# Two-layer transformer kernel: one DVE addition per rotation, key transposes in another PSUM pool, and a later place for the left factors of a seven-product multiplication

## The chip, the cores and the metric

The kernel runs on one core of a Trainium2 chip. The metric is the device time of one execution in microseconds, as the median of the runs shown. The engines have short names in the profile: PE is TensorE (matrix products), PEld its weight loads, DVE is VectorE, ACT is ScalarE, POOL is GpSimd, and SP is SyncE, whose queue issues all DMAs here.

## The reference

Two transformer layers over x of shape 4 x 256 x 256 (4 sequences, 256 positions, width 256), all in fp32. Each layer is `x = x + attention(layernorm(x))` followed by `x = x + ffn(layernorm(x))`.

```
# layer 0, attention: 16 query heads, 8 key/value heads of 128, window of 128
q, k, v = project(x)                       # per head: 256 -> 128
q, k = rms_norm(q), rms_norm(k)
q, k = rope(q), rope(k)                    # [x1*cos - x2*sin, x2*cos + x1*sin]
probs = softmax(mask(q @ k.T * scale));  out = (probs @ v) @ W_out
# layer 0, ffn: silu(x Wg) * (x Wu), keep the two largest of each four, times Wd
# layer 1, attention: 16 heads of 128, causal;  layer 1, ffn: silu(..)*(..), Hadamard transform, W2
```

What the change touches is the rotation and the key transpose in layer 0's attention, and the projections at the start of layer 1's attention.

## The kernel before, in words

**Stages.** The program runs `attention0`, `ffn0`, `attention1`, `ffn1` (lines 842 to 861), with overlaps at the seams. Layer 0's attention takes roughly the first 260 us, its FFN the time up to 367 us (the last products of it, `finish_ffn0`, run inside the next stage), layer 1's attention the time up to 660 us, and its FFN the rest.

**Units.** Each attention is cut into 16 units. In `attention0`, unit n belongs to sequence b = n // 4 and head group g = n % 4 (four query heads, two key heads, two value heads). `pipelined` (L301) runs six stages on them, each some steps behind the one before: `project` (no lag), `turn` (one step later), `score` (two), `split` (three), `join` and `attend` (four). So the step in which unit n is projected is also the one in which unit n-1 is turned and unit n-2 is scored.

**`project0` (L408)** multiplies the normalised input with the weights of a unit, for both halves t of the 256 positions. Each product of 128 x 512 lands in a PSUM tile `pj`, in the tag `half` of pool `ps2`, which has four buffers (L422). Two DVE multiplications read it, with the sines into `qs` and with the cosines into `qc` (L430); ACT squares it into `sq` (L435) and copies the values out (L437). After the products, DVE makes the rotation from two additions, one for each half of the 128 columns of a head (L441 and L442), and sums the squares (L443). POOL computes the reciprocal roots (L456 to L462) and scales the keys (L465). From unit 6 on (`by_dma`), POOL also splits the query words into two planes (L451) and a DMA transposes them (L453).

**`turn0` (L471)** brings queries and keys into transposed form. Up to unit 5 PE transposes the queries into a `half` tile (L478); from unit 6 on DVE copies the planes back (L485). The keys are always transposed by PE (L491) into a PSUM tile `tk` from `bank`, the tag of pool `ps1`, also with four buffers (L489), and ACT copies them out to `kT` (L492).

**Who else uses `bank`.** `probabilities` (L192) puts the scores `sc` there, one tile for each of a unit's four query heads, which DVE reads with a fused add-mask-and-maximum (L207) before ACT takes the exponentials (L217). `attend` (L374) takes two more for `av`, ACT copies them out (L388). A sequence's output projection `po` (L294) takes one, and a transposed input `tr_n` (L177) one.

**`attention1` (L656).** Each unit is projected with seven instead of eight block products (`seven_products`, L608): the left operand is the transposed input in four blocks and three combinations of them, which `left_of` (L588) makes with four DVE subtractions or additions (L596); the third of the seven products is the first to read a combination. The sums of the products are built by ACT copies (L613, L619, L622, L631) and DVE additions (L616, L625, L628). The four left operands are made in the first four units, in `project` (L659): unit b makes the operand of sequence b+1 and starts the normalisation of sequence b+2 (`normed`, L159, `by_dma`: DVE statistics and normalisation, two POOL instructions for the root, two POOL copies into planes, one transposing DMA issued by SP, two ACT copies out, L186), both before its own products.

**What sets the order.** Each engine executes its queue in order. The order within a queue is not that of the source: the build schedules the instructions of all engines by estimated readiness, subject to the dependencies, the free buffers and the order of the source. In the trace, for example, the products of unit 13 stand around the key transposes of unit 11. `tc.issue_after(ins)` adds one more constraint: instructions in its block come after `ins` on the same engine.

Of the kernel before, what the change touches and what calls it, by code (L numbers as in the profile page):

```python
# [24 lines left out]
ALU = mybir.AluOpType  # L25
# [23 lines left out]
def two_layers(ctx, tc, consts, tables, x, wq, wkv, wo, w_gate, w_up, w_down,  # L49
# [109 lines left out]
    def normed(b, factors=None, by_dma=False):  # L159

        mv, rstd = factors or moments(b)
        xnT = npool.tile([P, NC, T], F32, tag="xnT", name="xnT", bufs=4)
        if by_dma:
            planes = page_of_planes([P, NT, 2, D], "xpl")
        else:
            tr = bank([NC, T], "tr_n")
        for t in range(NT):
            cols = slice(t * P, (t + 1) * P)
            xn = npool.tile([P, D], F32, tag="xn", name="xn")
            last_of["norm"] = nc.vector.tensor_scalar(  # L170
                xn, xs[b * NT + t], mv[:, t, 0:1], rstd[:, t : t + 1], ALU.subtract, ALU.mult
            )
            if by_dma:
                copy_gpsimd(planes[:, t], xn.bitcast(U16).rearrange("p (n w) -> p w n", w=2))
                continue
            for c in range(NC):
                nc.tensor.transpose(tr[:, c, cols], xn[:, c * P : (c + 1) * P], ident)  # L177
        if not by_dma:
            nc.scalar.copy(xnT, tr)  # L179
            return xnT  # L180

        turned = page_of_planes([P, NT * 2 * NC, P], "xplT")
        nc.sync.dma_start_transpose(turned, planes.rearrange("p t w n -> p (t w n)"))
        for t in range(NT):
            cols = slice(t * P, (t + 1) * P)
            nc.scalar.copy(  # L186
                xnT[:, :, cols].bitcast(U16).rearrange("p c (n w) -> p c n w", w=2),
                turned[:, 4 * t : 4 * t + 4, :].rearrange("p (w c) n -> p c n w", w=2),
            )
        return xnT  # L190
# [125 lines left out]
    def attention0():  # L316
        with tc.tile_pool(name="attn0", bufs=2, reuse_waits="tile", side="right") as own:
            xnT, factors = {0: normed(0)}, {}


            cos_s = own.tile([P, NT, 2, HD], F32, name="cos_s", bufs=1)
            sin_s = own.tile([P, NT, 2, HD], F32, name="sin_s", bufs=1)
            with tc.issue_after(last_of["norm"].ins):
                for t in range(NT):
                    for tab, at in ((cos_s, 0), (sin_s, 256)):
                        src = angles[:, at + t * HD : at + (t + 1) * HD]
                        nc.vector.tensor_tensor(
                            tab[:, t], src.unsqueeze(1).to_broadcast([P, 2, HD]), scl, ALU.mult
                        )

            def project(n, _):
                b, g = divmod(n, 4)
                held = project0(own, xnT[b], g, cos_s, sin_s, n >= 6)
                if g == 1 and b + 1 < B:
                    factors[b + 1] = moments(b + 1)
                if g == 2 and b + 1 < B:
                    with tc.issue_after(last_of["qc"].ins):
                        xnT[b + 1] = normed(b + 1, factors[b + 1])
                return held

            def turn(n, held):
                rot, qT_planes, v, r = held
                return *turn0(own, rot, qT_planes), v, r

            def score(n, held):
                qT, kT, v, r = held
                ps = [
                    probabilities(
                        qT, kT, (2 * kk, 2 * kk + 1), mask0,
                        r[:, :, 2 * kk : 2 * kk + 2].rearrange("p t h -> p h t"),  # L350
                    )
                    for kk in range(2)
                ]
                return ps, v

            def split(n, held):
                ps, v = held
                return ps if n >= B * 4 - 3 else [
                    planes(p, own_planes) for p in ps
                ], v  # L360

            def own_planes(shape, name):
                return own.tile(shape, U16, tag="pl", name=name, bufs=4)

            def join(n, held):
                ps, v = held
                return [
                    transposed(ps[kk]) if n >= B * 4 - 3 else joined(ps[kk], ((
                        (nc.scalar.copy, slice(0, 2), last_of["exp"]),
                        (nc.scalar.copy, slice(0, 2), last_of["exp"]),  # L370
                    )[kk],)) for kk in range(2)
                ], v

            def attend(n, held):  # L374
                pTs, v = held
                zT = page("zT")
                for kk in range(2):
                    pT = pTs[kk]
                    av = bank([2, T], "av")
                    nc.tensor.matmul(  # L380
                        av, lhsT=v[:, 0, kk, :], rhs=pT[:, :, 0:T], start=True, stop=False,
                        skip_group_check=True,
                    )
                    nc.tensor.matmul(
                        av[:, :, P:T], lhsT=v[:, 1, kk, :], rhs=pT[:, :, T:],
                        start=False, stop=True, skip_group_check=True,
                    )
                    nc.scalar.copy(zT[:, 2 * kk : 2 * kk + 2, :], av)  # L388
                return zT

            def out(b, t, kept=False):
                def emit(done):
                    zTs = [done[4 * b + g] for g in range(4)]
                    if not kept:
                        project_out(bank([D], "po"), zTs, wo_sb, b, t)
                    else:
                        with tc.issue_after(last_of[0].ins):
                            project_out(half([D], "po"), zTs, wo_sb, b, t)
                return emit

            behind = {
                8: [out(0, 0)], 9: [out(0, 1)], 12: [out(1, 0)], 13: [out(1, 1)],
                17: [lambda _: xn_f.append(normed(0))],
                                19: [lambda _: xn_f.append(normed(1)), out(2, 0, True), out(2, 1, True), out(3, 0), out(3, 1)],
            }
            pipelined((project, turn, score, split, join, attend), (0, 1, 2, 3, 4, 4), behind, (0, 4, 3, 2, 1, 5))

    def project0(own, xnT, g, cos_s, sin_s, by_dma):  # L408
# [29 lines left out]
            rot.append((qc, qs, sq))  # L438
        for t, (qc, qs, sq) in enumerate(rot):

            nc.vector.tensor_tensor(qc[:, :, 0:64], qc[:, :, 0:64], qs[:, :, 64:], ALU.add)  # L441
            nc.vector.tensor_tensor(qc[:, :, 64:], qc[:, :, 64:], qs[:, :, 0:64], ALU.add)  # L442
            nc.vector.tensor_reduce(ss[:, t, :], sq, AX.X, ALU.add)  # L443
            rot[t] = qc
        qT_planes = None
# [22 lines left out]
            )  # L468
        return rot, qT_planes, v, r

    def turn0(own, rot, qT_planes):  # L471

        qT = page("qT")
        kT = own.tile([P, 2, T], F32, tag="kT", name="kT", bufs=3)
        for t, qc in enumerate(rot):
            cols = slice(t * P, (t + 1) * P)
            if qT_planes is None:
                tq = half([4, P], "tr_q")  # L478
                for j in range(4):
                    nc.tensor.transpose(tq[:, j, :], qc[:, j, :], ident)  # L480
                nc.vector.tensor_copy(qT[:, :, cols], tq)
            else:
                halves = qT_planes[:, 8 * t : 8 * t + 8, :]
                with tc.issue_after(last_of["mx"].ins):
                    nc.vector.tensor_copy(  # L485
                        qT[:, :, cols].bitcast(U16).rearrange("p j (c w) -> p j c w", w=2),
                        halves.rearrange("p (w j) c -> p j c w", w=2),
                    )
            tk = bank([2, P], "tr_k")  # L489
            for j in range(2):  # L490
                nc.tensor.transpose(tk[:, j, :], qc[:, 4 + j, :], ident)  # L491
            nc.scalar.copy(kT[:, :, cols], tk)  # L492
        return qT, kT
# [162 lines left out]
    def attention1(finish_ffn0):  # L656
        left = left1

        def project(n, _):  # L659
            g, b = divmod(n, 4)  # L660
            if g == 0 and b + 1 < B:
                left[b + 1] = left_of(xn1[b + 1])
            if g == 0 and b + 2 < B:
                xn1[b + 2] = normed(b + 2, by_dma=True)
            if b == 1 and 1 <= g < 3:
                load_group1(g + 1)
            return project1(left[b], gw[g])

        def score(n, held):
            qk, v = held  # L670
# [274 lines left out]
```

## Time and profile before

| | us |
|---|---|
| Median of 3 runs (lowest, highest) | 758.55 (758.15, 759.35) |
| The profiled execution, its own time | 761.02 |
| Its span, from the first to the last instruction | 759.2 |
| PE busy | 740.8 |
| DVE busy | 468.7 |
| ACT busy | 398.9 |
| POOL busy | 328.2 |
| DVE fused maximum on scores (L207), 256 instructions | 78.7 |
| POOL plane split of probabilities and inputs (L242), 54 | 80.1 |

A profile page gives busy times for an engine, the span in 40 slices with the busy share of each, the chain of work that ended last, and groups of instructions with their mean duration and the idle time before them. The views behind the page give waits ("engine, line, waited for: us in total, times, longest"), sums for any stretch of time, and the instructions in order of time ("start, us, engine, line, operation, output and input, shape, count, and in brackets the idle time before it and what ended it"). PE's matmuls are pipelined, so their durations overlap; what a matmul takes of PE's time is the distance from its start to the start of the next one. In this trace that distance, where nothing waits, is 0.429 us for a moving operand of 512 columns, 0.216 us for 256 and 0.112 us for 128 (medians). A `nc.tensor.matmul` in fp32 is two such instructions, a transpose one.

### The profile page before, as it was taken

How to read it: one execution, taken by the hardware profiler on the slowest of the kernel's cores; microseconds unless marked ns; L12 is line 12 of the kernel's file. 1: busy time of each engine (PE TensorE's matmuls, PEld its weight loads, DVE VectorE, ACT ScalarE, POOL GpSimd, SP SyncE). 2: the span in 40 equal slices, each digit the busy share in tenths (PEclk: the TensorE clock that was granted, in tenths of full speed). 3: DMA queues.
4: the chain of work that ended last, by engine and by line, in shares of the span. 5: the costliest groups of instructions: out<-in, count | busy, mean ns of one | idle time of the engine just before them, and what ended most of it. 6: DMA issues, size and time to landing. Idle time of an engine off the chain costs nothing. (4 is left out here: it accounts for less than half of the span.)

```text
span 759.2 us, 11685 instructions
## 1 busy us (share of the span) xinstructions
PE 740.8 (98%) x3980; PEld 602.5 (79%) x3980; DVE 468.7 (62%) x1428; ACT 398.9 (53%) x985; POOL 328.2 (43%) x475
## 2 busy tenths in 40 slices
PE   8999999998999999999989999999999999999998
PEld 5555556654666788888989999999998989899997
DVE  6999896699567515987655644464443447454433
ACT  2378886678558822222247555555555675415332
POOL 1588999779579301011116433343337645210000
PEclk9999999999999999999999999999999999999999
DMA  8724445426434050000433432342332222001100
GB/s 322 281 42 69 74 81 101 79 51 118 68 65 77 1 221 16 15 15 14 125 70 66 124 62 42 75 121 42 43 70 43 43 43 42 2 0 22 24 12 28
DMA packets 121611, 53.31 MB, mean 70 GB/s; under 512 B 114768, under 2 KB 116944, under 8 KB 120784
## 3 DMA queue, kind: packets, MB, share of 16 engines
q1 hardware_dynamic: 121552, 52.57, 30.1%
q8 instruction: 31, 0.51, 0.3%
q14 instruction: 28, 0.23, 0.1%
HBM read 22.94 MB, written 1.05 MB: 32 GB/s over the span
## 5 line engine op out<-in xcount | busy, mean ns | idle before, releaser
L225 POOL TENSOR_SCALAR p<-p,rs 128x128 f32<-128x128 f32 (+1 forms) x256 | 120.5, 488 | 159.9 <-DVE rs L222 156.6
L207 DVE CUSTOM_DVE_ANT_0 p<-sc,cst 128x128 f32<-128x128 f32 (+1 forms) x256 | 78.7, 349 | 10.4 <-PE sc L205 9.0
L242 POOL TENSOR_SCALAR pl<-p 128x1536 uint16<-128x1536 uint16 x54 | 80.1, 1483 | 8.2 <-DMA plT<-pl 4.1
L262 ACT COPY pT<-plT 128x768 uint16<-128x768 uint16 (+1 forms) x54 | 77.3, 1484 | 1.7 <-DMA plT<-pl 1.7
L217 ACT ACTIVATE p<-p,nb,r 128x128 f32<-128x128 f32 (+1 forms) x128 | 68.2, 536 | 10.1 <-DVE nb L214 10.1
L425 PE MATMUL pj<-wkv,xnT 128*128 128x512 f32 x128 | 62.7, 600 | 0.0
L425 PE MATMUL pj<-wq,xnT 128*128 128x512 f32 x128 | 60.8, 596 | 1.2 <-ACT xnT L179 0.7
L217 ACT ACTIVATE p<-p,nb 128x128 f32<-128x128 f32 (+1 forms) x128 | 56.3, 446 | 6.9 <-DVE nb L212 6.9
L155 POOL TENSOR_SCALAR ve<-mv 128x2 f32<-128x2 f32 x16 | 4.0, 248 | 124.4 <-DVE mv L152 124.1
L282 PE MATMUL po<-w_o,zT 128*128 128x256 f32 x256 | 57.7, 379 | 0.0
L294 PE MATMUL po<-wo,zT 128*128 128x256 f32 x256 | 57.2, 379 | 0.0
L294 PEld LDWEIGHTS po<-wo,zT 128*128 128x128 f32 x256 | 48.2, 190 | 6.3
L282 PEld LDWEIGHTS po<-w_o,zT 128*128 128x128 f32 x256 | 47.5, 190 | 5.8
L435 ACT ACTIVATE sq<-pj 128x512 f32<-128x512 f32 x64 | 30.0, 491 | 35.4 <-DVE qc L430 30.2
L425 PEld LDWEIGHTS pj<-wq,xnT 128*128 128x128 f32 x128 | 23.4, 190 | 24.7 <-issue 21.0
L425 PEld LDWEIGHTS pj<-wkv,xnT 128*128 128x128 f32 x128 | 23.7, 192 | 21.5 <-issue 20.1
L270 PE MATMUL av<-pT,v 128*128 128x256 f32 x128 | 38.8, 385 | 1.2 <-DVE mx L207 1.1
L205 PE MATMUL sc<-qk 128*128 128x256 f32 x128 | 38.2, 380 | 0.0
L205 PE MATMUL sc<-kT,qT 128*128 128x256 f32 x128 | 38.1, 381 | 0.0
L462 POOL TENSOR_TENSOR r<-ve,mhalf 128x12 f32<-128x12 f32 x16 | 37.2, 2322 | 1.3
L625 DVE TENSOR_TENSOR qk<-qk_y,u 128x512 f32<-128x512 f32 x16 | 11.1, 691 | 43.0 <-PE qk_y L738 40.0
L222 DVE RECIPROCAL rs<-sm 128x4 f32<-128x4 f32 x64 | 11.2, 175 | 41.5 <-ACT p L217 40.5
(155 smaller groups left out, 1784.9 us busy)
## 6 DMA issues: line engine op xcount, KB each, us to landing
w<-in_w_dram SPq DMA_DIRECT2D x3, 1024.0 KB, 4.8
wq<-in_wq_dram SPq DMA_DIRECT2D x4, 512.0 KB, 7.8
wkv<-in_wkv_dram SPq DMA_DIRECT2D x4, 512.0 KB, 8.3
wo<-in_wo_dram SPq DMA_DIRECT2D x4, 512.0 KB, 10.2
w_qk<-in_w_q_dram SPq DMA_DIRECT2D x4, 512.0 KB, 4.8
w_qk<-in_w_k_dram SPq DMA_DIRECT2D x4, 512.0 KB, 5.9
w_v<-in_w_v_dram SPq DMA_DIRECT2D x4, 512.0 KB, 7.0
w_o<-in_w_o_dram SPq DMA_DIRECT2D x4, 512.0 KB, 6.2
```

The source lines that it names most:

```text
L205: nc.tensor.matmul(sc[:, P : 3 * P], lhsT=q[:, P:T], rhs=k, start=True, stop=True)
L207: last_of["mx"] = nc.vector.tensor_tensor_reduce(out=p[:, j, cols], in0=sc[:, cols], in1=mask[:, cols], scale=1.0, scalar=-3.0e38, op0=ALU ...
L217: last_of["exp"] = nc.scalar.activation(p[:, j, cols], p[:, j, cols], AF.Exp, bias=nb[:, j, i : i + 1], scale=SCALE1 if rq is None else rq ...
L225: nc.gpsimd.tensor_scalar(p[:, j, cols], p[:, j, cols], rs[:, j, i : i + 1], 1.0, ALU.mult, ALU.mult)
L242: nc.gpsimd.tensor_scalar(o, i, 1.0, 1.0, ALU.mult, ALU.mult)
L262: copy(words.rearrange("p (n w) -> p w n", w=2), halves[:, :, js].rearrange("p w j n -> p w (j n)"),)
L270: nc.tensor.matmul(av, lhsT=v0, rhs=pT[:, 0:T], start=True, stop=False, skip_group_check=True)
L282: nc.tensor.matmul(po[:, t, :], lhsT=zT[:, j, t * P : (t + 1) * P], rhs=w[:, j, :], start=(t == j == 0), stop=(j == 3), skip_group_check=True,
L294: nc.tensor.matmul(po, lhsT=zTs[hd // 4][:, hd % 4, t * P : (t + 1) * P], rhs=w[:, hd, :], start=(hd == 0), stop=(hd == n - 1),)
L425: last_of[0] = nc.tensor.matmul(pj, lhsT=xnT[:, c, cols], rhs=w[:, g, c, :], start=(c == 0), stop=(c == NC - 1),)
L435: nc.scalar.activation(sq[:, hs], pj[:, 0:n], AF.Square)
L462: nc.gpsimd.tensor_tensor(r.rearrange("p t h -> p (t h)"), ve.rearrange("p t h -> p (t h)"), mhalf, ALU.pow)
```

## The change

There are three edits. The rotation's two additions become one over both halves of a head, whose second input runs through the halves in reverse order. `turn0` gets the function that allocates the key tile: `half` for units 6 to 13 (the 7th to the 14th), `bank` for the others as before. In `attention1`, `project` first issues its own products, then the left operand of the next sequence, behind the last DVE sum of these products, and then the normalisation of the one after; the loads of a later group's weights stay ahead of the products. One more line is only reformatted.

```
             def turn(n, held):
                 rot, qT_planes, v, r = held
-                return *turn0(own, rot, qT_planes), v, r
+                return *turn0(own, rot, qT_planes, half if 6 <= n < 14 else bank), v, r
...
-            nc.vector.tensor_tensor(qc[:, :, 0:64], qc[:, :, 0:64], qs[:, :, 64:], ALU.add)
-            nc.vector.tensor_tensor(qc[:, :, 64:], qc[:, :, 64:], qs[:, :, 0:64], ALU.add)
+            parts = [i.rearrange("p n (s h) -> p n s h", s=2) for i in (qc, qs)]
+            nc.vector.tensor_tensor(parts[0], parts[0], parts[1][:, :, ::-1, :], ALU.add)
...
-    def turn0(own, rot, qT_planes):
+    def turn0(own, rot, qT_planes, bank_of_k):
...
-            tk = bank([2, P], "tr_k")
+            tk = bank_of_k([2, P], "tr_k")
...
         def project(n, _):
             g, b = divmod(n, 4)
+            if b == 1 and 1 <= g < 3:
+                load_group1(g + 1)
+            held = project1(left[b], gw[g])
             if g == 0 and b + 1 < B:
-                left[b + 1] = left_of(xn1[b + 1])
+                with tc.issue_after(last_of["sum"].ins):
+                    left[b + 1] = left_of(xn1[b + 1])
             if g == 0 and b + 2 < B:
                 xn1[b + 2] = normed(b + 2, by_dma=True)
-            if b == 1 and 1 <= g < 3:
-                load_group1(g + 1)
-            return project1(left[b], gw[g])
+            return held
```

More of the change, by code (lines that the diff above doesn't have):

```diff
@@ L403, in attention0 @@
                 17: [lambda _: xn_f.append(normed(0))],
-                                19: [lambda _: xn_f.append(normed(1)), out(2, 0, True), out(2, 1, True), out(3, 0), out(3, 1)],
+                19: [lambda _: xn_f.append(normed(1)),
+                     out(2, 0, True), out(2, 1, True), out(3, 0), out(3, 1)],
             }
```

## The prediction, before the change was run

> **What bounds the kernel now.** I read the page's busy times first, then sums over stretches, then the waits, then single instructions around the places where PE waits.
>
> ```profile
> PE 740.8 (98%) x3980; PEld 602.5 (79%) x3980; DVE 468.7 (62%) x1428; ACT 398.9 (53%) x985; POOL 328.2 (43%) x475
> 20.00:120.00 100.00, 96.16 (x365) 55.90 (x364) 95.07 (x276) 72.59 (x186) 84.11 (x110) 1.00 0.45 105
> 120.00:240.00 120.00, 115.00 (x436) 75.44 (x435) 89.93 (x261) 80.76 (x191) 93.43 (x125) 0.99 0.43 79
> ```
>
> The first line is the page's, the others are sums over stretches (length, then PE, PEld, DVE, ACT, POOL busy, granted clock, DMA). PE sets the end: only its gaps can be won, never another engine's busy time as such. In layer 0's attention DVE is close behind: 95 of 100 us up to 120, 90 of 120 us after that.
>
> How large are the gaps? A busy PE is not PE at its peak, so I add up, for every matmul of the trace, the distance to the next start less the undisturbed distance of its form (0.429, 0.216 or 0.112 us). The sum over the span is 28.5 us. 4.1 of it fall before 20 us (start-up), about 16 between 20 and 262 us (layer 0's attention), 2.9 between 360 and 400 us, and 1.8 between 600 and 620 us. The waits view names the two largest releasers of PE:
>
> ```profile
> PE tr_k L491 <- DVE mx L207: 6.1, 6, 2.6
> PE qk_x L738 <- DVE qk L628: 1.6, 1, 1.6
> ```
>
> Key transposes wait for DVE's maxima, and one layer-1 product waits for a DVE sum. The key transposes need their inputs only from POOL's scaling L465, which ended 8 us or more before for every unit from 6 to 13 (L465's ends against L491's starts in the timeline). So the wait is for a `bank` that a score tile still holds. By start distances, the loss at units 6 to 13 is 0.56, 1.20, 1.09, 0, 0.76, 4.33, 0 and 0 us, together 7.94; unit 14, at 239.23, loses 1.28 and keeps its bank. The 4.33 are these lines of the timeline (PE, then DVE):
>
> ```profile
> 180.59 1.88 PE L425 MATMUL pj<-wq,xnT 128*128 128x512 f32 x4
> 185.09 1.21 PE L491 MATMUL tr_k<-cst,qc 128*128 128x128 f32 x4 [2.63 <-DVE mx L207]
> 181.57 0.28 DVE L207 CUSTOM_DVE_ANT_0 p<-sc,cst 128x128 f32<-128x128 f32 x1
> ...
> 181.78 1.50 DVE L441 TENSOR_TENSOR qc<-qc,qs 128x384 f32<-128x384 f32 x1
> 183.20 0.54 DVE L442 TENSOR_TENSOR qc<-qc,qs 128x384 f32<-128x384 f32 x1
> 183.67 0.94 DVE L443 TENSOR_REDUCE ss<-sq 128x6 f32<-128x768 f32 x1
> 184.53 0.41 DVE L207 CUSTOM_DVE_ANT_0 p<-sc,cst 128x256 f32<-128x256 f32 x1
> ...
> 184.60:188.10 3.50, 3.01 (x7) 1.74 (x8) 3.50 (x20) 2.31 (x9) 3.20 (x5) 0.51 1.11 202
> ```
>
> The four products started at 180.59 are through at 182.31 (4 x 0.429). The transposes need the bank of the first score tile, whose second maximum runs at 184.53, behind a rotation and a sum of squares: 2.79 us lost. The last line, a sum over 184.6 to 188.1, shows a granted clock of 0.51, which costs the other 1.54. Here row and rule differ: the Trainium skill (TensorE: Matmul & The Clock Gate, "Why this matters for your kernels") sees the clock fall after idle gaps above about 3 us. By that, this 2.8 us gap would cost 2.79 and the eight units 6.4; by the row it costs 4.33, and I take 7.94.
>
> **Part B, keys of units 6 to 13 in `half`.** No instruction is added; the wait on maxima goes. What is late next? A step allocates four `pj` and now two `tk` from four `half` buffers. I replayed each of the eight units with the releases of this trace (a `pj` is free after L430, L435 and, for keys and values, L437; a `tk` after L492).
> - Units 6, 7, 8, 12, 13: two or three buffers are free when the transposes come (unit 8: 129.9, 132.8 and 134.4 against 135.4), and the later `pj` find theirs. Loss 0.
> - Unit 9 (157.25, no loss now): both `tk` take the last free buffers; the next product, at 161.13, would wait for L492, which ends at 162.03: 0.9.
> - Unit 10: the second transpose waits for the `pj` released at 168.87 (ACT L437) instead of 168.2: about 0.65.
> - Unit 11: free buffers at 177.7, 180.8 and 183.1, so no wait before 183.1; then `attend` wants a bank, which the score tiles free from 184.9 on while PE's other work ends at about 184.9: 0.4.
> - A PE that arrives earlier meets DVE earlier: I add 0.65 for this, estimated as one more stall of unit 10's size.
>
> Back come 2.6 of 7.94: gain 5.3. Bounds: 8 (nothing comes back), and below nothing: see the slower rival.
>
> **Part A, one rotation sum.** 64 additions of 384 elements (rows of 0.54 us) become 32 of 768. L430's rows give 0.41 us for 256 and 0.68 for 512 elements, so 768 come to 0.95; the sum of squares L443, over 768, has 0.94. In distances between starts a pair takes 2 x 0.47 and the single one 0.87: 0.07 x 32 = 2.2 us of DVE. No row shows a reversed input; I take the cost as nothing, because its inner runs stay 64 elements long. If it ran at half speed, DVE would gain 32 x 0.9 = 29 us of work in the stage where it is 95% busy, and half of that could reach PE; I give this 0.02, within the slower case.
>
> Then the port. L441 and L442 together last 43.5 us against 64 x 0.543 = 34.8: 8.7 us too long, in 16 instructions, the longest ones (1.50 above, 1.81 at 177.12) ending 0.4 us after a POOL split L242 that had started before them. The Trainium skill (SBUF — State Buffer, "Who interferes with whom") has it that a DVE instruction with two SBUF inputs and a GpSimd one that reads SBUF exclude each other for a whole instruction. Half the instructions would, by the rule alone, be half the waits: 4.3 us. The rows say less: the 16 sit in 14 different pairs, and the joint addition meets the same POOL instruction; only the two doubled pairs are saved, about 1 us. The rule also speaks against the change: an addition that holds the port 0.94 instead of 0.54 us delays POOL. I take 1. So DVE is relieved by 3.2 us over 16 units; of this a quarter, 0.8, is on PE's path, by the 5 or 6 us of PE's loss in this stage that are neither key transposes nor start-up. Bounds 0 and 3.
>
> **Part C, left factors behind the sums.**
>
> ```profile
> 387.67 4.41 DMA xplT<-xpl
> 392.10 1.25 ACT xnT L186 x2
> 393.88 0.61 DVE qk L628
> 394.53 1.16 PE qk_x L738 x8
> ```
>
> This is the chain in order of time. The last sequence's normalised input arrives by DMA and ACT; DVE starts two L596 on it at 393.38, having stood idle 1.76 us for it with unit 1's sum L628 queued behind, and PE's last product of unit 1 waits for that sum: 1.79 us by start distance. With the edit, these L596 come behind unit 2's sums; L628 can run at about 391.7, and that stall goes. The second place is at 387.57: a value product waits for L616, which stands behind the normalisation L170 that waited 1.10 us for POOL's root: 0.58. `normed` now follows the products in the source; I take 0.4 of it. C gains 2.2.
>
> What is moved besides: six DVE statistics and normalisations, four POOL instructions (POOL idle 12.4 us there), one SP DMA (no weight load near it), two ACT copies L186. The operand of sequence 3 is read by unit 3's third product, at 412.04. Unit 2's sums end at 408.6; four L596 at 0.29 end at 409.8. Cover: 2.2 us. If L596 were planned behind the DVE copies L262, one of which waits for a DMA until 410.99, they would end near 413.8: stall 1.8 at 412.04, or 3.6 if PE comes 1.8 earlier, and C would be -1.2. Bounds 2.4 and -1.2.
>
> **Sum.** 5.3 + 0.8 + 2.2 = 8.3 us. The profiled execution's 761.02 (span 759.2 and 1.8 around it) becomes 752.7; it lay 2.5 above the median, so 758.55 becomes 750.3.
>
> **Rivals.**
> - *The wait moves to `av`.* The next taker of a `bank` in each step is `attend`, behind the same maxima. If it inherits the stalls, B gives nothing: 0.8 + 2.2 = 3.0, 755.5. For it: the score tiles hold all four banks. Against it: with PE's 1.7 us of `pj` work between, only unit 11 comes close.
> - *All stalls go*, and A's relief counts whole: 7.9 + 3 + 2.4, 745.3. Against it: DVE at 95%.
> - *Nothing reaches the end:* B moves, C loses as much as it wins: 758.
> - *Slower: `half` runs dry because ACT is late.* In the trace L492 for the second `tk` comes mostly 4.4 us after its transpose (157.5 to 161.9, 185.7 to 190.3), behind eight exponentials. A buffer held so long makes the next `pj` wait 0.9 as at unit 9. If this holds in eight units, it costs 7.2, on top of stalls moved to `av` (B's whole gain lost): 758.55 + 7.2 - 3.0 = 762.8. It decides from 0.4 us per unit on (3.0 / 8). Against it: L492 stands late where the transpose came late; an earlier transpose lets ACT copy first.
>
> **How the numbers follow.** Main case (747 to 753.5) 0.52; wait moves to `av` (753.5 to 757) 0.20; all stalls go 0.08; nothing reaches the end 0.09; slower 0.11. A measurement of this kernel can't tell less than 0.2% (1.5 us) from no change. The cases up to 757.0 are faster: 0.80; same 0.09; slower 0.11. The range 745.5 to 758.5 leaves out about half of the "all stalls go" case, a third of "nothing", and the slower case: some 0.18.
>
> **What would show it.** L441 alone, 32 times at 0.94 us, L442 gone; the wait of L491 on L207 down to unit 14's 1 us; clock 1.00 around 185; L425 waits on ACT below 3 us in total; no PE wait on L628 near 394 and none on L596 near 412. It is wrong if PE waits for L380 grow by as much as L491's shrink, or L425's on L492 do.

## The result, and the profile after

The changed kernel takes 755.38 us (median of 6 runs, 754.76 to 755.64); the kernel before took 759.22 beside it (6 runs, 758.15 to 761.08). The ratio is 0.9946, 95% interval 0.9932 to 0.9959. Repeated later it was 755.04 against 758.61: 0.9954 (0.9942 to 0.9966). So the gain is 3.6 to 3.8 us, 0.5%, where 8.3 us were forecast. The direction held, the time lies in the range, and the gain is less than half of the forecast. The line numbers after the edits are up to three higher than before: L441 became L443, L491 became L492, L425 L426, L616 L617, L628 L629, L738 L741.

The page's busy times:

```profile
PE 738.6 (98%) x3980; PEld 601.4 (80%) x3980; DVE 462.1 (61%) x1396; ACT 399.7 (53%) x985; POOL 330.0 (44%) x475
```

The sums over the same two stretches as before (length, then PE, PEld, DVE, ACT, POOL busy, granted clock, DMA):

```profile
20.00:120.00 100.00, 95.89 (x367) 56.39 (x366) 92.94 (x261) 73.68 (x191) 85.94 (x111) 1.00 0.47 107
120.00:240.00 120.00, 117.54 (x449) 77.27 (x448) 89.50 (x254) 84.39 (x201) 95.84 (x126) 1.00 0.45 81
```

DVE lost 32 instructions and 6.6 us. PE gained nothing up to 120 us and 2.5 us of busy time from 120 to 240, where the clock is now 1.00.

The loss of PE by start distances fell from 28.55 to 23.16 us. The difference, 5.39, is that of the two profiled executions (761.02 and 755.64). It has to be, since both kernels run the same matmuls; what the sum tells is where the time went. In layer 0's attention (20 to 262 us) it fell from 14.95 to 11.42, and from 360 to 420 us from 3.20 to 1.94. The waits view of the changed kernel (us in total, times, longest):

```profile
PE av L380 <- DVE mx L207: 3.5, 4, 1.5
PE av L270 <- DVE mx L207: 1.2, 1, 1.2
...
PE v_zy L747 <- DVE v L617: 0.7, 2, 0.4
...
PE pj L426 <- ACT sq L436: 0.6, 2, 0.4
...
PE qk_x L741 <- DVE qk L629: 0.2, 1, 0.2
```

The wait of the key transposes on maxima, 6.1 us before, is gone. The value products L380 now wait 3.5 us in four places, for the same maxima. Before, the same view had for them

```profile
PE av L380 <- DVE mx L207: 0.5, 1, 0.5
```

By start distances at units 6 to 13 (95 to 232 us, 8.03 us lost in all before), key transposes lost 6.83 us before and nothing now; value products lost 0.69 before and 4.55 now. One of the four places in order of time (lines of DVE and PE):

```profile
166.29 0.28 DVE L207 CUSTOM_DVE_ANT_0 p<-sc,cst 128x128 f32<-128x128 f32 x1
...
166.49 1.91 DVE L443 TENSOR_TENSOR qc<-qc,qs 128x768 f32<-128x768 f32 x1
...
166.74 0.60 PE L492 MATMUL tr_k<-cst,qc 128*128 128x128 f32 x4
...
167.18 1.02 PE L426 MATMUL pj<-wq,xnT 128*128 128x512 f32 x2
...
168.33 0.94 DVE L444 TENSOR_REDUCE ss<-sq 128x6 f32<-128x768 f32 x1
...
169.19 0.41 DVE L207 CUSTOM_DVE_ANT_0 p<-sc,cst 128x256 f32<-128x256 f32 x1
...
169.66 1.13 PE L380 MATMUL av<-pT,v 128*128 128x512 f32 x2 [1.46 <-DVE mx L207]
```

The key transposes run at 166.74 without a wait. After them stand only two products of the next unit, 0.86 us of work, and then `attend`, which wants the bank of the first score tile. That tile's second maximum runs at 169.19, behind the rotation sum and the sum of squares. It is the queue on DVE that held the keys up before; PE now meets it one group of products later.

The region of part C, DVE and PE in order of time:

```profile
383.54 0.42 DVE L617 TENSOR_TENSOR v<-v_zy,u 128x256 f32<-128x256 f32 x1
384.01 0.70 PE L747 MATMUL v_zy<-t_v,xs 128*128 128x256 f32 x2 [0.43 <-DVE v L617]
388.29 0.69 DVE L629 TENSOR_TENSOR qk<-qk_x,u 128x512 f32<-128x512 f32 x1 [0.23 <-PE qk_x L741]
389.18 1.05 PE L741 MATMUL qk_x<-xnT,t_qk 128*128 128x128 f32 x8
389.23 0.48 DVE L597 TENSOR_TENSOR xs<-xnT 128x128 f32<-128x128 f32 x2
```

The sum L629 of unit 1 no longer stands behind the left factors L597, and the product after it starts without a wait: the 1.79 us are gone. The wait for L617, which the prediction put at 0.58, is still there.

### The profile page after: what moved, and what is told of

Read it like the earlier page. It is cut to its first block, busy times and chain, and to the rows that moved or that the text cites. A ratio compares the mean times of both kernels' runs of the same rounds, so it can differ in the third digit from the quotient of the medians.

```text
span 753.8 us, 11642 instructions
## 1 busy us (share of the span) xinstructions
PE 738.6 (98%) x3980; PEld 601.4 (80%) x3980; DVE 462.1 (61%) x1396; ACT 399.7 (53%) x985; POOL 330.0 (44%) x475
## 5 line engine op out<-in xcount | busy, mean ns | idle before, releaser
L242 POOL TENSOR_SCALAR pl<-p 128x1536 uint16<-128x1536 uint16 x54 | 81.9, 1516 | 6.3 <-DMA plT<-pl 2.1
L426 PE MATMUL pj<-wq,xnT 128*128 128x512 f32 x128 | 61.8, 596 | 1.3 <-ACT xnT L179 0.7
L426 PE MATMUL pj<-wkv,xnT 128*128 128x512 f32 x128 | 60.9, 593 | 0.5 <-DMA wkv<-in_wkv_dram 0.5
L426 PEld LDWEIGHTS pj<-wkv,xnT 128*128 128x128 f32 x128 | 23.8, 190 | 27.8 <-issue 24.4
L426 PEld LDWEIGHTS pj<-wq,xnT 128*128 128x128 f32 x128 | 23.0, 190 | 22.0 <-issue 17.8
L632 ACT COPY qk<-qk_x 128x512 f32<-128x512 f32 x16 | 9.4, 586 | 53.8 <-PE qk_x L741 50.4
```

What stands on the lines that cost most here:

```text
L242: nc.gpsimd.tensor_scalar(o, i, 1.0, 1.0, ALU.mult, ALU.mult)
L426: last_of[0] = nc.tensor.matmul(pj, lhsT=xnT[:, c, cols], rhs=w[:, g, c, :], start=(c == 0), stop=(c == NC - 1),)
```

## The experiments

The question after the result: did B win nothing because its stalls moved to `av`, as the first rival has it, so that the gain comes from DVE's shorter work (A) and the one stall of C? Or did B win what the prediction said, and another edit, such as A's longer addition, take some of it back?

**The three edits singly, and rotation with keys.** All four ran on one chip beside the same 45 executions of before (758.77).

Rotation only is this edit, on the kernel before:

```
-            nc.vector.tensor_tensor(qc[:, :, 0:64], qc[:, :, 0:64], qs[:, :, 64:], ALU.add)
-            nc.vector.tensor_tensor(qc[:, :, 64:], qc[:, :, 64:], qs[:, :, 0:64], ALU.add)
+            nc.vector.tensor_tensor(parts[0], parts[0], parts[1][:, :, ::-1, :], ALU.add)
```

> The one rotation sum alone, on the kernel before. Theory 'inherited wait' (the key transposes' stalls mostly pass to the values' products, which need the same banks): the rotation sum shortens what stands between two maxima on DVE, and gains 0.5 to 1.5 us; the transposes still wait for maxima, 4 us or more in the waits view. Rival 'as forecast' (every term right, B only unlucky): 0.8. Rival 'the plan' (a shorter DVE instruction makes the build order the queues anew, and that is what matters): anything from -2 to +3 us, with a PE order that differs in many places.

Keys only:

```
-            tk = bank([2, P], "tr_k")
+            tk = bank_of_k([2, P], "tr_k")      # half if 6 <= n < 14 else bank
```

> Keys of units 6 to 13 in the projections' banks alone. 'Inherited wait': PE's wait of L491 on L207 falls below 1.5 us, that of L380 on L207 grows from 0.5 to 3 us or more; gain 1 to 2.5 us. 'As forecast': gain 5 us, L380's wait below 1 us.

Left factors only:

```
-                left[b + 1] = left_of(xn1[b + 1])
+                with tc.issue_after(last_of["sum"].ins):
+                    left[b + 1] = left_of(xn1[b + 1])
...
-            return project1(left[b], gw[g])
```

with the products issued ahead, as in the change.

> Left factors and normalisation behind the products alone. 'Inherited wait' (seen in the changed kernel's trace: the 1.8 us stall is gone, the 0.6 us one stays): gain 1.3 to 1.8 us. 'As forecast': 2.2, with no PE wait for a normalisation. If the edit also moves the plan of layer 0's attention, PE's loss before 262 us differs from that of before by over 0.5 us.

The first two edits together:

> Both edits of layer 0's attention, none of layer 1's. 'Inherited wait': the changed kernel's time plus 1.3 to 1.8 us, so 2 to 2.8 us below before. 'As forecast': 6.1 below before. If the sum of e1 and e2 differs from this by over 1 us, the two edits act through the plan and not each by itself.

| kernel | us (lowest to highest, runs) | ratio to before, 95% |
|---|---|---|
| rotation only | 756.19 (755.88 to 757.16, 8) | 0.9958 (0.9944 to 0.9972) |
| keys only | 757.83 (757.16 to 761.46, 22) | 0.9986 (0.9977 to 0.9996) |
| left factors only | 757.57 (756.56 to 760.10, 22) | 0.9985 (0.9974 to 0.9995) |
| rotation and keys | 755.73 (755.10 to 755.93, 6) | 0.9954 (0.9938 to 0.9969) |

So A gives 2.6 us, B 0.9 and C 1.2; the intervals of B and C reach nearly to no change. A gives more than either theory had for it (0.5 to 1.5, or 0.8). Nothing is taken back: A, which could have done that, is the largest part. Nor is there much of a new order of the queues behind A's gain: up to 262 us, only 10 of some 970 matmuls, and 10 of some 560 DVE instructions besides the additions, stand elsewhere than in before. Keys only, in the waits view:

```profile
PE av L380 <- DVE mx L207: 2.8, 5, 0.9
PE tr_k L491 <- DVE mx L207: 1.7, 2, 1.5
PE pj L425 <- ACT sq L435: 1.1, 3, 0.5
```

With no other edit, B alone moves the wait from the keys (6.1 before) to the value products (0.5 before) and a little to the projections. Here more than a quarter of these matmuls stand elsewhere: the build puts the transposes ahead of products that they stood behind. What is left on L491 belongs to units that keep their bank.

**The kernel before, profiled again.** Its profiled execution took 761.02, while more than half of its executions take 759 or less. I wanted to know whether the 4.33 us at unit 11 are there each time. It is the kernel before, unchanged.

> The kernel before, profiled once more. Theory 'one execution' (the 4.33 us at unit 11 belong to the profiled execution, not to the kernel): unit 11 loses about 1.1 us as in e3, whose instructions in layer 0's attention stand in the same order, the clock stays at 1.00 there, and the time is about 758; if it falls among the slow executions (760.4 and more, a third of the runs of before), the stall is above 2.5 us with a clock drop. Rival 'as forecast': 3 us or more lost there whatever the time.

This execution took 758.33 (span 756.5). The same place in order of time:

```profile
179.85 0.55 DVE L441 TENSOR_TENSOR qc<-qc,qs 128x384 f32<-128x384 f32 x1
180.32 0.55 DVE L442 TENSOR_TENSOR qc<-qc,qs 128x384 f32<-128x384 f32 x1
181.25 0.95 DVE L443 TENSOR_REDUCE ss<-sq 128x6 f32<-128x768 f32 x1 [0.39 <-ACT sq L435]
182.12 0.41 DVE L207 CUSTOM_DVE_ANT_0 p<-sc,cst 128x256 f32<-128x256 f32 x1
...
182.69 0.97 PE L491 MATMUL tr_k<-cst,qc 128*128 128x128 f32 x4 [0.59 <-DVE mx L207]
```

and the sum over 184 to 188 us:

```profile
184.00:188.00 4.00, 4.00 (x15) 2.59 (x14) 4.00 (x13) 3.15 (x12) 3.77 (x5) 1.00 0.56 101
```

In the first profile L441 lasted 1.50 us here, the transposes waited 2.63, and the clock fell to 0.51. In this execution both additions last 0.55, PE waits 0.59, and the clock stays at 1.00. In the first profile the delay begins one rotation earlier (POOL and DVE in order of time):

```profile
176.88 1.65 POOL L242 TENSOR_SCALAR pl<-p 128x1536 uint16<-128x1536 uint16 x1
177.12 1.81 DVE L442 TENSOR_TENSOR qc<-qc,qs 128x384 f32<-128x384 f32 x1
181.41 1.47 POOL L242 TENSOR_SCALAR pl<-p 128x1536 uint16<-128x1536 uint16 x1
```

and the same L442 in this one:

```profile
176.46 0.55 DVE L442 TENSOR_TENSOR qc<-qc,qs 128x384 f32<-128x384 f32 x1
```

Both long additions of the first profile (1.81 and 1.50) run beside a POOL split. In this execution unit 11 loses 1.06 us, and unit 12, which lost nothing in the first, 0.92. The sum of losses is 25.85 us instead of 28.55: 2.70 less, which is the difference of the two times (2.69). At units 6 to 13 it is 5.75, not the 8.03 of the first profile. So the profile that I worked from held a stall that the program doesn't always have.

The times of all executions beside the experiments say how often. In 28 of 91 executions of the kernel before, the mean granted clock is below 0.9985, and these take 760.38 to 761.77; the other 63 take 757.57 to 759.76, with nothing in between. (The six beside the result, whose clock is not on record, include one of 760.01.) The profiled one (761.02, clock 0.997) is of the first kind. With keys only it is one execution of 22, with left factors only 6 of 22, and none of the 37 of the five kernels that hold the rotation edit without a further cost (rotation only, rotation and keys, rotation and left factors, the changed kernel in both measurements, and the one with values in `half`). That each of the 28 loses its clock at unit 11 isn't shown: one execution of that kind was profiled.

This bears on the single gains too. Among executions whose clock stays at 0.9985 or more, the medians are 758.27 before, 756.19 with rotation only, 757.75 with keys only, 757.39 with left factors only and 755.73 with rotation and keys. So A gives 2.1 us, B 0.5, C 0.9, and A with B 2.5; the changed kernel gives 3.4 (755.04 against 758.46 in its second measurement). These gains add up to within 0.1 us.

**Rotation and left factors, without the keys** (the change with `bank` for all keys), and **values in `half` too**, on one chip beside 11 executions of before (759.29). The second adds to the change:

```
+                pool_of = half if 3 <= n < 11 else bank
...
-                    av = bank([2, T], "av")
+                    av = pool_of([2, T], "av")
```

> The changed kernel with its key transposes back in `bank` for all units: rotation and left factors only. If keys are worth little once the rotation is one sum ('inherited wait'): 0.2 to 0.8 us slower than the changed kernel, so 3 us below before. If keys carry the gain: 3 us slower than the changed kernel.

> The changed kernel, with the values' products of the same steps (units 3 to 10) in `half` as well. 'Inherited wait': PE's 3.5 us of L380 waiting for maxima go at these units; up to 3 us faster than the changed kernel if nothing takes their place. Rival 'half runs dry': six more takers of four buffers, the projections wait for ACT or DVE for 3 us or more, and the time is the same or 2 to 5 us longer.

Without the keys the time is 755.84 (755.41 to 756.54, 6 runs; ratio 0.9950, 0.9936 to 0.9965). The changed kernel's own ratios, 0.9946 and 0.9954, lie inside that interval: on top of A and C, part B can't be told from nothing. In its waits view the old wait is back:

```profile
PE tr_k L491 <- DVE mx L207: 4.5, 5, 1.4
```

At units 6 to 13 the loss by start distances is 4.95 us without the keys and 5.10 with them: on top of A and C, B moved its stalls and took nothing away there. What differs is the stretch from 232 to 262 us, 3.00 without and 2.33 with keys in `half`, mostly at unit 14's transposes (1.58 and 0.61), which B doesn't move; why they wait less is not shown.

With values in `half` too the time is 754.42 (754.35 to 754.67, 5 runs; ratio 0.9931, 0.9917 to 0.9945), and the waits view has

```profile
PE pj L427 <- ACT zT L389: 2.7, 2, 1.8
...
PE av L381 <- DVE mx L207: 1.5, 1, 1.5
```

The wait has moved a second time, now to products that want a `half` buffer which ACT hasn't copied out. At units 6 to 13 the loss is 3.66 us (5.10 in the changed kernel). This version beats both kernels in its median; over the changed one it is 0.6 to 1.0 us, not measured side by side, with overlapping intervals.

**Rotation behind the maxima.** If the maxima come too late because the rotation stands ahead of them, turn the order round. The additions, the sums of squares, the roots and the scalings become a stage of their own, on top of the change:

```
+            def rotate(n, held):
+                after = last_of.get("mx")
+                with tc.issue_after(after.ins) if after else nullcontext():
+                    return rotate0(*held)
...
+            pipelined((project, rotate, turn, score, split, join, attend), (0, 0, 1, 2, 3, 4, 4), behind, (0, 5, 4, 3, 1, 2, 6))
```

> The changed kernel, with the rotation sums and sums of squares of a unit on DVE behind the maxima of the same step. If what L380 waits for is the DVE queue's order (a rotation sum and a sum of squares between the two maxima of the first score tile), its wait on L207 falls from 3.5 us to below 1.5, and the kernel is 1 to 3 us faster than the changed one. Rival: the later sums delay POOL's planes and scalings, PE waits for keys and queries instead, and it is 1 to 5 us slower.

770.88 us (770.38 to 772.97, 4 runs; ratio 1.0152, 1.0133 to 1.0171). That is some 15 us slower than the changed kernel, where the rival had 1 to 5. The wait of L380 on the maxima is gone from the view, so their cause was named rightly, but the first line is now

```profile
PE tr_k L501 <- POOL qc L475: 15.1, 9, 4.0
```

The keys need POOL's scaling, which needs the sums. In its profiled execution the mean granted clock is 0.991, so part of the loss is clock. The sums and the maxima are due within the same stretch on DVE, which is busy for all of the 8 us from 164 to 172 in the changed kernel. In both orders tried, what stands second is waited for; less work on DVE (A) shortened the waits, another order did not.

**The normalisation forced behind the sums.** The 0.58 us of C stayed because the build still plans the normalisation ahead of L617. Forced, on top of the change:

```
-                xn1[b + 2] = normed(b + 2, by_dma=True)
+                with tc.issue_after(last_of["sum"].ins):
+                    xn1[b + 2] = normed(b + 2, by_dma=True)
```

It ran with the changed kernel, with this edit on top of values in `half`, and with the rotation cut in four, on one chip beside 35 executions of before (758.61).

> The changed kernel once more, as the measure for the three that run beside it: 755.0 to 755.8, 3 to 4 us below before.

> The changed kernel, with the two normalisations of layer 1's start held behind the sums as well. If the remaining 0.59 us near 384 is DVE waiting in its queue for POOL's root (the part of C that was forecast to go and didn't), it is gone and the kernel is 0.4 to 0.7 us faster than e9. Rival: the later normalised inputs make the left factors or the products of units 2 and 3 late, 0.5 us or more slower than e9.

> e10 with the values of units 3 to 10 in the projections' banks (as e7). If the two act in different stages and each by itself: 1.3 to 1.8 us faster than e9, near 753.9. If not: as e7, 754.4, or slower.

The changed kernel again 755.04 (754.88 to 755.62, 6 runs). The forced one 758.48 (757.17 to 759.02, 14 runs; ratio 0.9988, 0.9977 to 0.9999), 3.4 us slower. It was expected to be 0.4 to 0.7 us faster. The wait for L617 near 384 us is gone, but this came instead (POOL, SP's queue, ACT and PE in order of time):

```profile
391.98 1.23 POOL L242 TENSOR_SCALAR xpl<-xn 128x512 uint16<-128x512 uint16 x2 [0.60 <-issue]
393.24 1.23 SPq L183 DMA_TRANSPOSE xplT<-xpl  x1
396.30 1.25 ACT L186 COPY xnT<-xplT 128x512 uint16<-128x512 uint16 x2 [1.66 <-DMA xplT<-xpl]
399.71 0.56 ACT L614 COPY u<-qk_x 128x512 f32<-128x512 f32 x1
400.33 1.16 PE L742 MATMUL qk_x<-xs,t_qk 128*128 128x128 f32 x8 [2.35 <-ACT u L614]
```

The input of sequence 3 leaves DVE later, so its DMA lands later. ACT's copies L186 wait for it at 396.30, with exponentials and L614 queued behind, and PE waits 2.35 us for L614. It is the kind of loss that the prediction's lower bound for C feared of DVE's queue, on ACT's. The five executions whose granted clock stays above 0.9985 (757.17 to 757.35) are 2.2 us slower than the changed kernel, about this wait; in the other nine the clock is lower, and they take 758.18 to 759.02.

With values in `half` on top it took 757.25 (755.67 to 758.88, 22 runs; ratio 0.9977, 0.9968 to 0.9987), so these don't mend it. Half of these executions, too, show a clock below 0.9985. The profiled one, 758.88, shows the same gap of PE (2.3 us) with another end, in the sum over 400 to 404 us:

```profile
400.00:404.00 4.00, 3.98 (x17) 3.62 (x18) 1.28 (x5) 2.41 (x10) 3.91 (x6) 0.57 0.43 80
```

The clock is 0.57 after this gap; in the profile of the forced edit alone (757.29) it is 1.00 over the same stretch.

**The rotation in four additions** on the kernel before, to size what DVE's time is worth to PE from the other side:

```
+            for hs in (slice(0, 3), slice(3, 6)):
+                nc.vector.tensor_tensor(qc[:, hs, 0:64], qc[:, hs, 0:64], qs[:, hs, 64:], ALU.add)
+                nc.vector.tensor_tensor(qc[:, hs, 64:], qc[:, hs, 64:], qs[:, hs, 0:64], ALU.add)
```

> The kernel before, with each rotation's sum in four additions of 192 elements instead of two of 384. If the one sum gains by DVE's time and by fewer meetings with POOL at the port, four lose by the same: DVE 4 to 8 us more busy and the kernel 1.5 to 3 us slower than before, above all between 20 and 262 us. If the gain of the one sum came from a luckier order of the queues, four are anywhere between 2 us faster and 5 slower, without relation to DVE's time.

766.40 us (765.70 to 767.40, 5 runs; ratio 1.0105, 1.0089 to 1.0121). Its page:

```profile
PE 738.4 (97%) x3980; PEld 600.6 (79%) x3980; DVE 482.7 (63%) x1492; ACT 398.5 (52%) x985; POOL 326.1 (43%) x475
```

and its waits:

```profile
PE tr_k L492 <- DVE mx L207: 10.7, 8, 1.7
PE tr_n L177 <- DVE xn L170: 3.3, 4, 1.2
```

DVE is busy 14.0 us more than in the first profile of before, and the end comes 7.8 us later; 4 to 8 and 1.5 to 3 were expected. The largest part is the same wait, grown from 6.1 to 10.7; PE's wait for the normalised input grew from 0.4 to 3.3. Most of the added loss, 7.7 us, falls between 20 and 95 us. More than a quarter of the matmuls up to 262 us stand in another order than before, so how much is DVE's time alone and how much the order is not shown.

## Why the prediction was right in direction and wrong in size

- **What bounds the kernel: right.** PE's gaps set the end, and in layer 0's attention DVE's queue ends most of them. (The "about 16" us between 20 and 262 are 14.95 by the same sum.)
- **B, the stall of 7.94 us: mis-sized.** Two executions without the long stall (before again, and left factors only, which has the same queues there) lose 5.7 to 5.8 us at these units. 761.02 lay above the median because of this very stall. I subtracted the 8.3, in which it is counted whole with its 1.54 us of lost clock, from the median as well: some 2.3 us of the gain (8.03 less 5.75) were in the profile and not in most of the runs that make the median. Between clock rule and row I chose the row; it was a true row of one execution, of a kind that makes up about a third. For the median, even the rule's 6.4 was too much.
- **B, "only unit 11 comes close": the step that failed.** I put the stalls that `attend` inherits at 0.4 us; the value products lose 4.55 in the changed kernel, against 0.69 before. I replayed the `half` buffers unit by unit, and they held: waits of L426 on ACT's squares are 0.6 us in all. I did not replay `bank` for `attend` in the same way; I only asked when PE's other work would end at unit 11, with PE's order as it was. In the changed kernel the build puts the transposes right after the scores, no longer behind four products as at 180.59 before, and `attend` follows after two products (0.86 us), while the second maximum comes 2.45 us after the transposes (169.19 against 166.74). The first rival, to which I gave 0.20, is what happened: its price for B, nothing, is near the measured 0.9 alone and the unresolved remainder on top of A and C. That its 755.5 lies beside the measured 755.38 is luck: A gave 1.8 us more than it had, C 1.0 less, and before itself was 0.7 slower than the 758.55 it started from.
- **A, 0.8 us: too small.** Measured alone: 2.6, or 2.1 without the executions whose clock fell. What was mis-sized is DVE's relief, put at 3.2. *The port:* I counted two saved meetings, 1 us, where my estimate from the rule of the Trainium skill (SBUF — State Buffer, "Who interferes with whom"), that such an addition and a reading GpSimd instruction exclude each other, was half of 8.7 for half the instructions. The excess over undisturbed durations is 8.7 and 7.9 us in the two profiles of before, 4.85 with rotation only (35.06 less 32 x 0.944), 6.4 in the changed kernel, and 9.7 with values in `half` too. So half was nearer for rotation only, the changed kernel lies between, and in the last the excess is no smaller than before: it depends on how the queues meet, not on the number of additions alone. *The share on the path:* with 2.2 from start distances, rotation only won DVE about 5.3 us (2.2 + 7.9 - 4.85). 2.1 is 0.4 of that, and PE's loss in layer 0's attention fell by 1.75 (13.27 in before again, 11.52), a third. The quarter was somewhat low, and its reason was wrong: half of the 1.75 came at units 6 to 13, on the key waits that I had left out. The key waits are DVE's waits too.
- **A, reversed input: right.** The joint addition takes 0.94 us at its shortest, as the sum of squares does.
- **C, 2.2 us: half.** The 1.79 at 394 went as worked out, and nothing came late at 412. The 0.4 at 384 did not come, since the order in the source didn't change the build's plan there, and two waits of 0.38 (372.4) and 0.30 (406) came up: 1.79 less 0.68 is 1.1, measured 1.2 (0.9 without the executions whose clock fell).
- **The slower rival** (`half` runs dry): 0.6 us of such waits; it would have needed 7.2.
- **The sum.** 2.6 + 0.9 + 1.2 = 4.7 singly, 3.6 to 3.8 together. This is not a sign that the edits work on the same waits: the third of before's executions with a fallen clock lifts its median, and every single gain counts that. Without them it is 2.1 + 0.5 + 0.9 = 3.5 against 3.4. What stays open is what B's remainder of about 0.5 us rests on; it lies below what the runs resolve.

## What to carry to other kernels

When a buffer holds up one consumer, find the instruction that frees it, and list everybody who takes a buffer freed by the same instruction in the next few microseconds: moving one of them only helps if the next is later than the release. The build may put the moved one ahead of work that it stood behind, so replay the next taker in the new order. When the releaser is an engine without a gap at that place, its own work is the currency; here about 0.3 to 0.4 of what was won there reached the end. Before a gain read from one profile is subtracted from a median, compare the profiled execution with the median; if it lies above, look for the stall that puts it there, and leave it out.

## What the hardware showed that I had not expected

- PE gaps of the same length ended in different clocks. After 2.6 us of idle the clock fell to 0.51 in one execution of before; after 2.4 us it stayed at 1.00, and after 2.3 us it fell to 0.57, in two kernels with the forced normalisation (there alone, and with values in `half`). By the mean clock of whole executions, it fell in 9 of 14 of the first of these and in 11 of 22 of the second. The Trainium skill (TensorE: Matmul & The Clock Gate, "What's actually happening") has a free-running window of about 3.4 us, after an idle one of which the clock falls; these gaps are shorter than that window, and the clock still fell.
- The same program runs in two groups of times (28 and 63 of 91 executions), their medians 2.3 to 2.9 us apart in the three sets of runs, which the granted clock divides without exception. In the one profile of the longer kind the stall begins with two additions beside POOL splits that last 1.81 and 1.50 instead of 0.55 us; that this is how each of the 28 begins was not tried.
- A longer addition still meets POOL: 1.91 us instead of 0.94 at 166.49, until 0.8 us after the POOL split L242 that began at 166.13 and lasted 1.47 had ended.
